# A vision tower on one core: value weights turned a unit sooner, a gate behind the last image's rows, the last tile's output on two queues

## The chip, the cores and the metric

The kernel runs on one core of a Trainium2 chip. The metric is the device time of one execution in microseconds (us). The kernel before was timed in 14 runs: median 732.39 us, from 729.04 to 736.07 us.

The core has five engines with their own instruction streams, each of which is executed strictly in its written order: TensorE (PE in the profile: matrix products and transposes), VectorE (DVE), ScalarE (ACT: activations and copies), GpSimd (POOL: here mostly transfers with row indices) and SyncE (SP: issues transfers). They wait for each other through semaphores. An engine whose next instruction waits holds up everything behind it, though that may be ready.

## The reference

Everything is float32. Four images of 224 x 224 become 784 patches each; the tokenizer gives tokens of 256 numbers, and since query, key and token are the same tokens joined, every row occurs three times (the kernel computes it once). Two layers follow.

```python
h = tokenizer(x)                                    # (4, 3*784, 256)
h = h + L0_attn(layernorm(h))
h = h + L0_ffn(layernorm(h))
h = h + L1_attn(layernorm(h))
h = h + L1_ffn(layernorm(h))

def L0_attn(m):                # attends over the 4 images, for each position and head
    mn = layernorm(m); q, k, v = mn @ Wq, mn @ Wk, mn @ Wv
    g = sigmoid(mn @ Wg + bg)
    att = softmax(einsum('slhc,tlhc->sth', q, k) * scale, axis=1)
    o = einsum('sth,tlhc->slhc', att, v) * g
    return o @ Wo + bo

def L0_ffn(f):                 # 6 experts of three layers, the best 2 of each row
    logits = softmax(relu(f @ router_w1 + router_b1) @ router_w2 + router_b2)
    top_w, top_i = top_k(logits, 2)
    return sum over the two of softmax(top_w) * expert[top_i](f)

def L1_attn(x):                # linear attention: no product of rows with rows
    q, k, v = split(x @ W_qkv + b_qkv)
    q, k = q - mean(q), k - mean(k)
    k2 = l2_normalize(k*k / (sum(k*k) + eps), axis=rows)
    q2 = l2_normalize(q*q / (sum(q*q) + eps), axis=columns)
    return (v + q2 @ (k2.T @ v) / sqrt(N)) @ W_out + b_out

def L1_ffn(x):                 # a shared MLP and the best 2 of 4 small experts
    return shared(x) + sum over the two of weight * expert(x)
```

## The kernel before, in words

**Tiles.** The 784 rows of an image are six tiles of 128 rows and 16 rows left over. The leftovers of all four images share one more tile, number 24 (`LT`), in four bands of 32 partitions. So there are 25 tiles, and `h` (all rows, 256 numbers each) stays on the chip from the tokenizer to the output.

**Order.** Large stretches stand under `tc.manual_schedule`, in which the named engines execute their instructions in the order in which the program writes them. Elsewhere, and for an engine that a stretch doesn't name, a scheduler chooses the order, and it may put such instructions between those of a stretch ordered by hand.

**Layer 0 attention, last image (lines 1575 to 1681).** `s` is image 3, the last; `u` is the unit of six tiles of image 2, whose rows are normalised (`rows_of_part`, line 1025, on ACT), transposed (`turn_part`, lines 311 and 1039) and given to the router while image 3 attends. For image 3, `gate_mm(s, o)` has computed two halves of the gate on PE, `gate_act(s, o)` (line 896) takes their tanh on ACT. The weights of the four images come from `shares_before` and `shares_after` (lines 928 to 937; an exponential on ACT, the rest on DVE). `first_value` (lines 953 and 955) writes the first of four weighted value terms, on the engine that it is given, and `values` (lines 960 and 965) adds the other three and multiplies by the gate, on DVE. The columns are taken in two pieces, the first 512 (`GN`) and the remaining 272 (`rest`). Then `attended` (line 989) multiplies by `Wo` on PE, adds to `h` on DVE and squares on ACT (line 995); `scales_of` takes the roots (line 1004), `shifts_of` the factors on DVE (line 1009).

**Layer 0 experts.** Rows are sent to a table in memory, sorted by expert, by POOL (`send`, line 1154, two transfers a tile), and fetched in blocks of 256 rows (`load`, line 1498). The weights of a block's expert are copied to a buffer (`own_weights`, line 1519, DVE), the block is transposed (line 1528), taken through two layers (`hidden`, line 1543 on PE, line 1549 on ACT) and a third (`rows_back`, line 1561), and stored. Blocks 0 to 6 start while images 2 and 3 are still being routed. `mix1` to `mix3` (lines 1284 to 1295) compute the mixing weights; they are written later, in a stretch that orders DVE, SP and POOL by hand but not ACT.

**Layer 1 attention, start (from line 2207).** Units are three tiles, `LU` is the unit of tile 24 alone. For each unit PE computes q and k (`qk_mm`, line 2001), DVE adds the bias (`qk_add`, line 2007), ACT squares (`qk_squares`, lines 2015 and 2016) and takes roots (`root`, line 2033), DVE makes factors (lines 2039 to 2043) and scales q (`q_rows`, line 2055), ACT scales k (`k_rows`, line 2048). Meanwhile `stats_one` (lines 1767 to 1785) adds the experts' rows to the next unit on DVE, `norm_root` (line 1797) takes its root on ACT, and `norm_rows` (lines 1806 and 1809) normalises on DVE. The value weights never meet the rows directly: `layer1_weights` folds them with `W_out`. It is a generator, run one step at a time with `next(steps)`:

```python
    step 1:  PE transposes Wv (line 812); ACT copies two biases (818) and the result, WvT (819)
    step 2:  PE multiplies WvT by Wout into pwvo (825); ACT copies the two halves to Wvo (829)
    step 3:  PE multiplies the bias (834); ACT copies it (835); DVE adds it to bout (837)
```

Before the change, steps 1 and 2 stand around unit `LU`'s transposes, after all squares of units 0 and 1. `Wvo` is first read by `rows_out` (line 2180).

**Layer 1 experts and output (lines 2326 to 2425).** Seven parts: four of four tiles, then three of three (16 to 18, 19 to 21, 22 to 24). After each part DVE adds the result to `h` (line 2415), and each tile is written to the output three times over (line 2423): 384 KB by SP, or, for the odd tile of the last part, by ACT. Tile 24 goes out as four pieces of 16 rows, one an image.

Of the kernel before, what the change touches and what calls it, by code (L numbers as in the profile page):

```python
# [28 lines left out]
TT = 128  # L29
# [43 lines left out]
def tile_vit_tower(ctx: ExitStack, tc: tile.TileContext, a: dict, out: bass.AP):  # L73
# [819 lines left out]
    def gate_act(s, o):  # L893
        gate = gates[s, o] = attr.tile([P, SEQ], F32, tag="gate", name="gate")
        for i, pg in enumerate(pgs.pop((s, o))):
            nc.scalar.activation(
                gate[:, i * HALF : (i + 1) * HALF], pg, AF.Tanh, bias=bgh[:, o : o + 1], scale=0.5
            )
# [22 lines left out]
    def shares_before(s):  # L921
        if s not in pls:
            shares_mm(s)
        pl = pls.pop(s)
        plv = pl[:, : 2 * NI].rearrange("p (o t) -> p o t", t=NI)
        w = atts[s] = small.tile([P, 2, NI], F32, tag="att", name="att")
        mx = small.tile([P, 2], F32, tag="mx0", name="mx0")
        nc.vector.tensor_reduce(mx, plv, AX.X, ALU.max)
        nc.vector.tensor_tensor(w, plv, mx.unsqueeze(2).to_broadcast([P, 2, NI]), ALU.subtract)
        nc.scalar.activation(w, w, AF.Exp, scale=scale)  # L930
        return mx
# [649 lines left out]
    with tc.manual_schedule(engines=by_hand | {ENG.SP}):  # L1581
        gate_mm(s, 0)
        gate_mm(s, 1)
        products(s, 1, [1])
        expert_weights([2])
        scales_of(u)
        steps = early_blocks()
        next(steps)
        products(s, 1, [2])
        shifts_of(u)  # L1590
        next(steps)
        gate_act(s, 0)
        products(s, 1, [3])
        expert_weights(range(3, E0))
        next(steps)
        mx = shares_before(s)
        next(steps)
        gate_act(s, 1)
        shares_after(s, mx)
    att.close()  # L1600
    work[0] = layer0.enter_context(tc.tile_pool(name="blocks", bufs=2, reuse_waits="tile"))
# [4 lines left out]
    )  # L1606
    with tc.manual_schedule(engines=by_hand | {ENG.SP}):
        first_value(s, 0, 0, GN, nc.vector)
        first_value(s, 1, 0, GN, nc.scalar)
        rows_of_part(u)  # L1610
        values(s, 0, 0, GN)
        for _ in steps:
            pass
        for i in range(4):
            load(i)
        values(s, 1, 0, GN)
        turn_part(u)
        for o in range(2):
            first_value(s, o, *rest, nc.scalar)
        router(u)  # L1620
        values(s, 0, *rest)
        values(s, 1, *rest)
        attended(s, [0, 1])
        keep_left(s)
        attended(s, [2, 3])
        scales_of(ua)
        router_logits(u)
        shifts_of(ua)
        for i in (0, 1):
            b = cols[:, rows[f"eb{i + 1}_0"] :][:, : 2 * E0].rearrange("p (e r) -> p e r", r=2)  # L1630
            nc.vector.tensor_copy(ew[:, :, 6 * D + 2 * i : 6 * D + 2 * i + 2], b)
        attended(s, [4, 5], 0)
        own_weights(0)
        rows_of_part(ua)
        attended(s, [6])
        hidden(0, 0)
        turn_part(ua)
        own_weights(1)
        scales_of(ub)
        choose(u)  # L1640
        turned(1)
        shifts_of(ub)
        rows_of_part(ub, both=True)
        router(ua)
        count(u)
        send(u)
        hidden(0, 1)
        turn_part(ub, both=True)
        router_logits(ua)
        own_weights(2)  # L1650
        hidden(1, 0)
        rows_back(0)
        load(4)
        choose(ua)
        router(ub)
        turned(2)
        hidden(1, 1)
        count(ua)
        hidden(2, 0)
        send(ua)  # L1660
        rows_back(1)
        load(5)
        router_logits(ub)
        own_weights(3)
        turned(3)
        hidden(2, 1)
        choose(ub)
        hidden(3, 0)
        rows_back(2)
        load(6)  # L1670
        own_weights(4)
        count(ub)
        turned(4)
        hidden(3, 1)
        send(ub)
        hidden(4, 0)
        rows_back(3)
        own_weights(5)
        turned(5)
        steps = later_blocks()  # L1680
        hidden(4, 1)
        next(steps)
        hidden(5, 0)
        next(steps)
        rows_back(4)
        next(steps)
        load(7)
        load(8)
        own_weights(6)
        turned(6)  # L1690
        hidden(5, 1)
        next(steps)
        hidden(6, 0)
        next(steps)
        rows_back(5)
        load(9)
        hidden(6, 1)
# [332 lines left out]
    def root(u):  # L2030
        n = units[u][2]
        s4 = sumsof[u][1]
        nc.scalar.activation(s4[:, :n], s4[:, :n], AF.Sqrt, bias=zero[:TT])
# [177 lines left out]
    with tc.manual_schedule(engines=by_hand | {ENG.Pool}):  # L2211
        x_t(1)
        for j in range(UT):
            qk_mm(0, j)
            qk_add(0, j)
            qk_squares(0, j)
        root(0)
        for j in range(UT):
            qk_mm(1, j)
        qk_add(1, 0)  # L2220
        qk_squares(1, 0)
        stats_one(LU, 0)
        norm_root(LU)
        factors(0)
        qk_add(1, 1)
        qk_squares(1, 1)
        norm_rows(LU)
        for b in range(NI):
            nc.gpsimd.tensor_scalar(
                xaM[:, b, :], xaL[:, 0, : D + 2], ofimage[:, b : b + 1], None, ALU.mult  # L2230
            )
        fetch(3)
        qk_add(1, 2)
        qk_squares(1, 2)
        root(1)
        q_rows(0)
        stats_one(2, 0)
        next(steps)
        x_t(LU)
        q_t(0)  # L2240
        k_rows(0)
        next(steps)
        stats_one(2, 1)
        factors(1)
        q_rows(1)
        k_rows(1)
        qk_mm(LU, 0)
        stats_one(2, 2)
        norm_root(2)
        next(steps)  # L2250
        Wvo, bvo = lw[:2]
        q_t(1)
        qk_add(LU, 0)
        qk_squares(LU, 0)
        root(LU)
        norm_rows(2)
        squares[0] = k_squares(0)
        factors(LU)
        fold(0, squares.pop(0))
        k_rows(LU)  # L2260
        squares[LU] = k_squares(LU)
        q_rows(LU)
        squares[1] = k_squares(1)
        fold(1, squares.pop(1))
        k_x_tiles(0)
        x_t(2)
        k_x_left(0)
        kn = k_norm(0)
        fetch(4, kn[:1, :1])
        k_x_out(0, kn)  # L2270
        qk_mm(2, 0)
        qk_add(2, 0)
        qk_squares(2, 0)
        stats_one(3, 0)
        qk_mm(2, 1)
        qk_add(2, 1)
        qk_squares(2, 1)
        q_t(LU)
        gT = g_t(0)
        stats_one(3, 1)  # L2280
        qk_mm(2, 2)
        qk_add(2, 2)
        kv_out(0, gT)
        qk_squares(2, 2)
        stats_one(3, 2)
        normalise(3)
        fetch(5, xa_of(3)[:1, 0, :1])
        rows_out(0)
        x_t(3)
        root(2)  # L2290
        factors(2)
        k_rows(2)
        q_rows(2)
        for j in range(2):
            qk_mm(3, j)
            qk_add(3, j)
            qk_squares(3, j)
            stats_one(4, j)
        squares[2] = k_squares(2)
        qk_mm(3, 2)  # L2300
        qk_add(3, 2)
        qk_squares(3, 2)
        stats_one(4, 2)
        root(3)
        norm_root(4)
        norm_rows(4)
        fetch(6, xa_of(4)[:1, 0, :1])
        parts_ = rows_out_parts(1)
        next(parts_)
        fold(2, squares.pop(2))  # L2310
        factors(3)
        k_rows(3)
        q_t(2)
        x_t(4)
        for done in parts_:
            pass
        q_rows(3)
        squares[3] = k_squares(3)
        fold(3, squares.pop(3))
        behind.append(done.ins.name)  # L2320
# [38 lines left out]
    with tc.tile_pool(name="ffn1", bufs=2) as work:  # L2359
# [3 lines left out]
        for g, tiles in enumerate(parts):  # L2363
# [50 lines left out]
            for j, t in enumerate(tiles):  # L2414
                nc.vector.tensor_tensor(h[:, t, :], pms[j], h[:, t, :], ALU.add)
                b, i = divmod(t, TPI)

                eng = nc.scalar if g == len(parts) - 1 and j % 2 else nc.sync
                cuts = [(b, i * TT, 0, TT)]
                if t == LT:  # L2420
                    cuts = [(k, TPI * TT, k * SEG, LEFT) for k in range(NI)]
                for k, s0, p0, rows_ in cuts:
                    eng.dma_start(
                        out=out[k].rearrange("(k s) d -> s k d", k=REP)[s0 : s0 + rows_],
                        in_=h[p0 : p0 + rows_, t, :].unsqueeze(1).to_broadcast([rows_, REP, D]),
                    )
# [33 lines left out]
```

## Time and profile before

| | us |
|---|---|
| median of 14 runs | 732.39 |
| the profiled execution | 733.89 |
| its span, first to last instruction | 732.2 |
| PE busy in the span | 689.6 |
| DVE busy | 459.5 |
| ACT busy | 332.1 |
| POOL busy | 128.8 |
| mean granted clock of PE | 0.987 |

The profile is of one execution. A timeline line gives the start of an instruction or of several alike (us from the start of the span), how long they took together, the engine, the line of the code, the operation, what it writes and reads, and how many there are; a bracket at its end gives the idle time of the engine just before and what ended it, as far as semaphores show. "issue" stands for a wait for which the profile shows no cause. A matrix product in float32 is recorded as two passes, so eight records are four products. In the table of stretches, a line gives the stretch, its length, the busy time of PE, its weight loads, DVE, ACT and POOL (with the number of instructions begun there), the granted clock of PE, the busy share of the 16 DMA engines and GB/s. The chain of waits goes back from the last instruction, at each step to what released it.

### The profile page before, as it was taken

How to read it: one execution, taken by the hardware profiler on the slowest of the kernel's cores; microseconds unless marked ns; L12 is line 12 of the kernel's file. 1: busy time of each engine (PE TensorE's matmuls, PEld its weight loads, DVE VectorE, ACT ScalarE, POOL GpSimd, SP SyncE). 2: the span in 40 equal slices, each digit the busy share in tenths (PEclk: the TensorE clock that was granted, in tenths of full speed). 3: DMA queues.
4: the chain of work that ended last, by engine and by line, in shares of the span. 5: the costliest groups of instructions: out<-in, count | busy, mean ns of one | idle time of the engine just before them, and what ended most of it. 6: DMA issues, size and time to landing. Idle time of an engine off the chain costs nothing.

```text
span 732.2 us, 9849 instructions
## 1 busy us (share of the span) xinstructions
PE 689.6 (94%) x3043; PEld 477.0 (65%) x3043; DVE 459.5 (63%) x1385; ACT 332.1 (45%) x816; POOL 128.8 (18%) x242
## 2 busy tenths in 40 slices
PE   6899999999997897999999999997999999999996
PEld 4655656566655686788888866664776855555553
DVE  6576775869988733357556668685968654354441
ACT  1665665566797652323332338463545232222231
POOL 6400000000075256200003318453000000000000
PEclk9999999999999899999999999999999999999999
DMA  5999998000037724223234432121000013322333
GB/s 181 313 426 425 425 425 363 0 1 0 1 122 218 278 94 143 96 87 94 94 111 135 120 117 79 55 73 56 1 1 1 4 30 120 118 92 54 115 105 96
DMA packets 56476, 96.49 MB, mean 132 GB/s; under 512 B 6696, under 2 KB 46350, under 8 KB 56424
## 3 DMA queue, kind: packets, MB, share of 16 engines
q1 hardware_dynamic: 49924, 79.69, 30.4%
q0 software_dynamic: 5600, 14.32, 6.5%
q10 hardware_dynamic: 900, 1.86, 0.8%
q8 instruction: 24, 0.39, 0.2%
q14 instruction: 28, 0.23, 0.1%
HBM read 30.75 MB, written 65.09 MB: 131 GB/s over the span
## 4 chain that ended last, share of the span: by engine, by line
PE 58%; DVE 4%; ACT 2%; issue 1%; DVEq 0%; ACTq 0%
PE pb L1543 13%; PE pe L320 6%; PE pyb L1561 6%; PE ps L320 5%; PE pqk L2001 4%; PE ps L2410 3%; PE pukx L2100 3%; PE pout L2180 3%; PE pout L2185 3%; PE pt L311 2%; PE pe L2380 2%; PE ps L2404 2%; PE ptb L1528 1%; PE pkvo L2160 1%; ACT qk L2015 1%
## 5 line engine op out<-in xcount | busy, mean ns | idle before, releaser
L1154 POOL DMA_INDIRECT xrows<-xn,pos x50 | 54.8, 1097 | 212.7 <-DVE nm L1010 172.7
L1753 POOL DMA_INDIRECT ys<-yrows,pos x50 | 49.4, 988 | 134.4 <-DMA yrows<-yb 120.0
L1549 ACT ACTIVATE hb<-pb,own 128x256 f32<-128x256 f32 (+1 forms) x74 | 33.5, 457 | 58.0 <-PE pb L1543 36.8
L1543 PE MATMUL pb<-xTb,own 128*128 128x256 f32 (+1 forms) x240 | 54.5, 371 | 4.9 <-DVE own L1519 2.3
L1543 PE MATMUL pb<-hb,own 128*128 128x256 f32 (+1 forms) x240 | 54.5, 368 | 0.3 <-DVE hb L1551 0.2
L1561 PE MATMUL pyb<-own,hb 128*128 128x256 f32 x216 | 52.3, 381 | 0.3 <-ACT hb L1549 0.2
L1543 PEld LDWEIGHTS pb<-xTb,own 128*128 128x128 f32 x240 | 43.0, 195 | 11.2 <-ACT xn L1025 2.6
L320 PE MATMUL pe<-xT,eW 128*128 128x512 f32 (+1 forms) x112 | 46.0, 553 | 0.0
L2001 PE MATMUL pqk<-Wqkv,lxT 128*128 128x512 f32 x100 | 45.0, 595 | 0.2 <-ACT lxT L94 0.2
L1543 PEld LDWEIGHTS pb<-hb,own 128*128 128x128 f32 x240 | 41.5, 194 | 5.1 <-DVE hb L1551 0.9
L1561 PEld LDWEIGHTS pyb<-own,hb 128*128 128x128 f32 x216 | 40.1, 190 | 6.3 <-ACT hb L1549 1.1
L1567 DVE TENSOR_TENSOR yb<-pyb,eb 128x512 f32<-128x512 f32 (+1 forms) x30 | 19.1, 638 | 37.2 <-PE pyb L1561 31.8
L637 PE MATMUL pw<-Wall,pT 128*128 128x512 f32 (+1 forms) x96 | 42.4, 592 | 0.0
L1532 ACT COPY xTb<-ptb 128x512 f32<-128x512 f32 (+1 forms) x30 | 16.3, 542 | 54.1 <-PE ptb L1528 46.0
L907 DVE SCALAR_TENSOR_TENSOR prod<-kq 128x784 f32<-128x784 f32 x32 | 30.6, 969 | 7.3 <-ACT kq L882 3.9
L320 PEld LDWEIGHTS pe<-xT,eW 128*128 128x128 f32 x112 | 20.2, 190 | 21.6 <-issue 16.5
L1519 DVE COPY own<-kq 128x1540 f32 x30 | 29.2, 976 | 6.6 <-ACT xTb L1532 3.1
L311 PEld LDWEIGHTS pt<-ident,xn 128*128 128x128 f32 x200 | 24.6, 146 | 12.9 <-issue 9.7
L637 PEld LDWEIGHTS pw<-Wall,pT 128*128 128x128 f32 (+1 forms) x96 | 17.9, 189 | 20.5 <-issue 18.5
L2001 PEld LDWEIGHTS pqk<-Wqkv,lxT 128*128 128x128 f32 x100 | 18.6, 192 | 19.4 <-issue 17.5
L1551 DVE TENSOR_SCALAR hb<-pb,own 128x256 f32<-128x256 f32 (+1 forms) x46 | 20.3, 445 | 17.4 <-PE pb L1543 16.5
L311 PE MATMUL pt<-ident,xn 128*128 128x128 f32 x200 | 28.9, 284 | 2.1 <-issue 1.8
(420 smaller groups left out, 1441.1 us busy)
## 6 DMA issues: line engine op xcount, KB each, us to landing
xrows<-nothing SPq DMA_DIRECT2D x22, 896.0 KB
yrows<-nothing SPq DMA_DIRECT2D x22, 896.0 KB
out_dram<-h SPq DMA_DIRECT2D x23, 384.0 KB
xb<-xrows SPq DMA_DIRECT2D x24, 256.0 KB
yrows<-yb SPq DMA_DIRECT2D x24, 256.0 KB
kq<-in_L_ffn_expert_w_dram SPq DMA_DIRECT2D x18, 256.0 KB
wb<-wd SPq DMA_DIRECT2D x16, 128.0 KB
img<-in_x_dram SPq DMA_DIRECT2D x5, 294.0 KB
```

The source lines that it names most:

```text
L311: nc.tensor.transpose(pt[:, j * TT : (j + 1) * TT], xn[:, j, c * P : (c + 1) * P], ident[:TT, :TT])
L320: nc.tensor.matmul(pm[: wcols.stop - wcols.start, :n], w[:, c, wcols], xT(c), start=(c == 0), stop=(c == chunks - 1),)
L637: nc.tensor.matmul(pm, pixels(c, tiles[j]), Wall[: K1[c], c, :], start=(c == 0), stop=(c == 1))
L907: nc.vector.scalar_tensor_tensor(prod, qTs[s][:, o, :], 1.0, kT[:, o, t * SEQ : (t + 1) * SEQ], ALU.mult, ALU.mult, accum_out=atts[s][:, o ...
L1154: put = nc.gpsimd.indirect_dma_start(out=xrows[:, :], out_offset=bass.IndirectOffsetOnAxis(ap=pos[:, k, t0 + j : t0 + j + 1], axis=0), in_ ...
L1519: nc.vector.tensor_copy(w, ewf[0][:, bass.ds(off, EW)])
L1543: nc.tensor.matmul(pm, wm[:, c, o * P : (o + 1) * P], src[:, c, :], start=(c == 0), stop=(c == 1),)
L1549: nc.scalar.activation(dst[:, o, :], pm, AF.Relu, bias=b)
L1561: nc.tensor.matmul(pm[:, t, :], src[:, c, t * P : (t + 1) * P], wm[:, c, :], start=(c == 0), stop=(c == 1),)
L1753: got = nc.gpsimd.indirect_dma_start(out=y[:, j, k, :], out_offset=None, in_=yrows[:, :], in_offset=bass.IndirectOffsetOnAxis(ap=pos[:, k, ...
L2001: nc.tensor.matmul(pqk, xTs[u][:, c, cut(j, 1)], Wqkv[:, c, : 2 * D], start=(c == 0), stop=(c == 1),)
L2100: nc.tensor.matmul(pg, uks[u][:, k, c * P : (c + 1) * P], xas[u % 4][:, k, : D + 2], start=(j == 0), stop=False,)
```

## The change

Three edits. The first moves the second gate of the last image behind the rows of `u` and their transposes, and spreads these rows differently. The second runs steps 1 and 2 of `layer1_weights` earlier: step 1 after unit 0's squares, step 2 after unit 1's products. The third adds a case that cuts the last tile of the last part in two halves, and a line that gives every piece of that tile but the first to ACT. The last tile of the last part is tile 24, `LT`.

```diff
@@ -1593,9 +1593,9 @@
         products(s, 1, [3])
         expert_weights(range(3, E0))
         next(steps)
+        rows_of_part(u, part=(0, 1))
         mx = shares_before(s)
         next(steps)
-        gate_act(s, 1)
         shares_after(s, mx)
...
         first_value(s, 0, 0, GN, nc.vector)
+        rows_of_part(u, part=(1, 4))
         first_value(s, 1, 0, GN, nc.scalar)
-        rows_of_part(u)
+        rows_of_part(u, part=(4, TPI))
         values(s, 0, 0, GN)
         for _ in steps:
             pass
         for i in range(4):
             load(i)
+        turn_part(u)
+        gate_act(s, 1)
         values(s, 1, 0, GN)
-        turn_part(u)
         for o in range(2):
             first_value(s, o, *rest, nc.scalar)
...
             qk_squares(0, j)
+        next(steps)
         root(0)
         for j in range(UT):
             qk_mm(1, j)
+        next(steps)
         qk_add(1, 0)
         qk_squares(1, 0)
...
         stats_one(2, 0)
-        next(steps)
         x_t(LU)
         q_t(0)
         k_rows(0)
-        next(steps)
         stats_one(2, 1)
...
                 if t == LT:
                     cuts = [(k, TPI * TT, k * SEG, LEFT) for k in range(NI)]
+                elif t == parts[-1][-1]:
+                    cuts = [(b, i * TT + p, p, TT // 2) for p in (0, TT // 2)]
                 for k, s0, p0, rows_ in cuts:
+                    if t == parts[-1][-1] and p0:
+                        eng = nc.scalar
                     eng.dma_start(
```

## The prediction

> **What bounds the kernel now.** I read the page first: TensorE (PE) is busy 94% of the span and the chain that ended last lies on it for 58%, so an edit counts only where PE waits for it, or where it moves what PE waits for.
>
> ```profile
> span 732.2 us, 9849 instructions
> PE 689.6 (94%) x3043; PEld 477.0 (65%) x3043; DVE 459.5 (63%) x1385; ACT 332.1 (45%) x816; POOL 128.8 (18%) x242
> PE 58%; DVE 4%; ACT 2%; issue 1%; DVEq 0%; ACTq 0%
> ```
>
> Then the timelines of the three places that the diff touches. Place 1, last image of the attention: ScalarE (ACT) with its second gate ahead of the six rows, then VectorE (DVE), then PE.
>
> ```profile
> 232.53 1.05 ACT L896 ACTIVATE gate<-pg,bgh 128x392 f32<-128x392 f32 x2
> 233.47 0.72 ACT L953 ACTIVATE oT<-vT,att 128x512 f32<-128x512 f32 x1
> 234.08 3.05 ACT L1025 ACTIVATE xn<-h,nm,r 128x256 f32<-128x256 f32 x6
> 240.56 0.94 ACT L953 ACTIVATE oT<-vT,att 128x272 f32<-128x272 f32 x2
> ```
> ```profile
> 239.25 0.69 DVE L965 SCALAR_TENSOR_TENSOR oT<-gate,oT 128x512 f32<-128x512 f32 x1
> 241.13 1.58 DVE L960 SCALAR_TENSOR_TENSOR oT<-vT,att,oT 128x272 f32<-128x272 f32 x3 [1.18 <-issue]
> ```
> ```profile
> 252.44 3.44 PE L1543 MATMUL pb<-xTb,own 128*128 128x256 f32 x8 [2.25 <-DVE own L1519]
> ```
>
> DVE stands 1.18 us before its last value products, until ACT has written their first terms (240.56). From there one string runs: h additions 245.06, ACT squares 245.52, root 249.33, expert weights 251.33, and PE's first expert block at 252.44 after 2.25 us of nothing.
>
> Place 2, start of layer 1: ACT squares two units of rows without a pause, and only then copies the turned value weights, for which PE waits at 447.19.
>
> ```profile
> 440.27 0.30 ACT L2033 ACTIVATE s<-s,zero 128x3 f32<-128x3 f32 x1
> 440.65 0.42 ACT L2015 ACTIVATE qk<-qk 128x256 f32<-128x256 f32 x1
> 442.24 0.30 ACT L1797 ACTIVATE rstd<-mv,eps 128x1 f32<-128x1 f32 x1 [0.29 <-DVE mv L1785]
> 446.57 0.58 ACT L819 COPY WvT<-pwv 128x512 f32<-128x512 f32 x1
> ```
> ```profile
> 443.15 0.60 PE L812 MATMUL pwv<-ident,Wqkv 128*128 128x128 f32 x4
> 447.19 3.68 PE L825 MATMUL pwvo<-Wout,WvT 128*128 128x256 f32 x8 [0.98 <-ACT s L2033]
> 461.50 3.68 PE L2001 MATMUL pqk<-Wqkv,lxT 128*128 128x512 f32 x8
> ```
>
> Place 3, the end: SyncE issues five output DMAs from 726.19 on, and the DMA engines are full until 730.
>
> ```profile
> 726.19 3.58 SPq L2423 DMA_DIRECT2D out_dram<-h  x5
> ```
> ```profile
> 728.00:729.00 1.00, 0.00 (x0) 0.00 (x0) 0.00 (x0) 0.00 (x0) 0.00 (x0) 1.00 0.99 314
> 729.00:730.00 1.00, 0.00 (x0) 0.00 (x0) 0.00 (x0) 0.00 (x0) 0.00 (x0) 1.00 0.99 220
> 730.00:731.00 1.00, 0.00 (x0) 0.00 (x0) 0.00 (x0) 0.00 (x0) 0.00 (x0) 0.82 0.58 152
> ```
>
> **Place 1, step by step.** In the built streams only ACT changes here; DVE, PE, POOL and SP keep their order. ACT is free at 231.66 and waited 0.76 us for the shares' exponential at 232.41; row 0 (0.51 us) fits into that. Rows 1 to 3 then end at 234.06, the first term at 234.7, rows 4 and 5 at 235.7 (24 rows in 12.7 us). PE turns rows as they come, so the four copies (2 x 0.55, 0.65 together) run 235.6 to 237.1. The gate, now behind them, runs to 238.1; its reader on DVE is at 239.25, a margin of 1.1 us. The first terms follow until 239.0, before DVE wants them at 239.9. So the 1.18 us go, and nothing else is late (none of the moved steps issues a DMA): PE's router products start 2 us sooner, half of them at the low clock, and PE's next rows are ready at 243.7 where DVE now comes at 243.9. The string up to PE's block moves by **-1.18**: 251.26.
>
> The streams show one more thing that the diff does not: ACT's later work that no hand orders (exponentials of the mixing weights, L1284, L1285) is scheduled differently. The first now stands between the two halves of the first block's relu, ahead of the root (L1004). That makes two more table loads, 1.28 us each (the load at 258.32 moves up; one is added before the root, one before L1285). ACT has idle time for them: 1.23 us before the second half, 1.98 us before the next block's relu at 265.02. Counting from PE's block, the second half goes from +3.47 to +3.7, the root from +5.1 to +6.6, so DVE's last row ends at +7.85 where the scatter's places were computed at +7.72: +0.16. Rows, router and second layer stay at +7.3, +8.3, +8.9. Bounds: 0 (all in idle time) to 2.57 (both in the open); I take **+0.16**, since the idle rows are longer than the loads.
>
> [...]
>
> After that comes a standstill: DVE waits 7.04 us ("remote") to 278.08, ACT 5.27 us to 278.83, while POOL scatters until 277.0 and PE has nothing. Its end coincides with the end of the scatters, which start from DVE's places at 260.7, so I let the gain through: 0 to -1.02, taken **-1.0**. If the first block also escaped the low clock (clock 0.50 at 253 to 256, 3.44 us for what takes 1.73 elsewhere) it would be -2.7.
>
> **Place 2.** PE transposes the value weights after unit 0's six products instead of after unit 1's, and multiplies them (pwvo) right after unit 1's. That removes the 0.98 us wait and, with PE dense, the low clock (3.68 us against 1.73 for eight such passes): 2.7 us to gain on PE. But ACT must copy them in its own order. Its stream is now: squares of unit 0 (end 440.23), two bias copies, WvT copy (end 441.2), root (441.5), **both Wvo copies (L829), then the squares of unit 1**. The copies wait for pwvo, and pwvo for unit 1's products: 432.85 + 12 x 0.858 + 0.43 for the transposes = 443.58, first half done at 444.45. So ACT stands about 3.0 us, copies at 444.5 and 445.4 (0.37 each), and squares unit 1 from 445.65 instead of 440.65. Queued behind: the root of the left unit (L1797), 442.24 to 446.9. For it DVE waits in norm_rows: its reciprocal goes from 443.32 to 447.2, **+3.88**. Behind that on DVE are the last addition of unit 1, the q rows, three tiles' statistics, factors and q rows of unit 1; DVE was busy 11.76 of 13 us there, so it can't catch up. What it regains is its 1.36 us wait for the bias copy L835 at 453.90, of which 0.66 go (ACT needs root and copy after 456.4: 457.1 against 453.9): +3.22 at the next unit's rows and at the folded sums, which end 463.4 instead of 460.2. PE needed them at 460.69, a slack of 0.5. Its products of unit 2 start at 464.3 instead of 461.50: **+2.8**. On POOL the left unit's masks (L2229) start at 447.85 instead of 446.18, and the three tiles' fetches behind them end at 458.6, early enough for DVE at 467. PE's own way there is shorter (pukx from 455.3 behind q rows, 453.94 before), with 1.3 us to spare for a low clock. Bounds: -2.7 (the stall is hidden, PE keeps its gain) to +3.9 (DVE's whole shift).
>
> **Place 3.** The last tile is the one with the four images' left rows, so the test t == LT comes first and the halves of 64 rows are never cut. What the diff does is send images 1 to 3 (48 KB each) from ACT, behind its 384 KB; nothing else is queued there. SP's issues were at 727.06, 727.46, 727.93 and 729.29, the third taking 1.36; now all are out by about 728.4. But the DMA engines were full to 730 and 0.58 busy after; packing the rest tightly gives 0.2. Bounds: +0.3 (three issues of 0.4 behind ACT's own, last at 728.3, with a 1.36 in it) to -0.9 (the last issue's 1.36 less 0.48). Taken: **-0.2**.
> [...]
>
> **Sum.** -1.0 + 2.8 - 0.2 = +1.6. The profiled execution took 733.89 (span 732.2 and 1.69 around it), 1.50 above the median of the 14 runs. +1.6 makes it 735.5, and the median 732.39 becomes **734.0**.
>
> **Rivals.**
> 1. *The standstill eats place 1* (slower). At 271 to 278 ACT and DVE wait for something that the trace does not name. If its end isn't tied to the scatters, an earlier start buys nothing: 0 + 2.8 - 0.2 = +2.6, 735.0, slower by 0.36%. It decides from the point where DVE's wait grows by as much as its arrival is sooner. For it: no semaphore from POOL stands there. Against: the scatters end 1.1 us before. ACT's longer stream could also lengthen its wait.
> 2. *The stall of place 2 is half hidden.* If the work behind PE at 461 can absorb it, place 2 is 0: -1.2, 731.2. For it: PE reads pwvo's result only at 470. Against: DVE is 90% busy.
> 3. *Place 2 gains as it was drawn*: -1.0 - 2.7 - 0.2 = -3.9, 728.5. It needs ACT to hold unit 1's squares ahead of the copies; the built stream has them behind.
>
> **Chances.** A measurement of this kernel can tell about 0.3% (2.2 us) from no change, and +1.6 lies inside. Forecast 0.56 (its own range 732.6 to 735.6; 0.16 of it above +2.2), rival 1 and what is worse than it 0.24, rival 2 0.10, rival 3 0.10. Faster 0.10, within 0.50, slower 0.40. The range leaves out rival 3 and the worst of the first (both places at their upper ends, +6): 730.6 to 736.8.
>
> **What would show it.** Place 1: the gate behind the xT copies, no wait before L960 on 272 columns, the first pb 1.2 us sooner, loads before L1004 and L1285. Place 2: ACT idle about 3 us before L829, DVE's reciprocal of the left unit waiting 3 to 4 us for ACT, pwvo in 1.7 us, the unit-2 products 2 to 3 us later relative to the first pqk. Place 3: three issues on ACT after 727.03, data ending within 0.3 us of where it did. I am wrong if DVE does not wait there, or if the distance from the first pb to the first pqk changes by over 1 us.

## The result and the profile after

The changed kernel took **744.50 us** (median of 13 runs, 739.69 to 747.43) beside 733.03 us for the kernel before (62 runs): a ratio of 1.0150, 95% interval 1.0134 to 1.0166, some 11 us slower. The forecast was 734.0, its range ended at 736.8, and its sign was right with a chance of 0.40 only.

The page after, the same three lines as before:

```profile
span 739.0 us, 9857 instructions
PE 696.1 (94%) x3043; PEld 479.4 (65%) x3043; DVE 459.4 (62%) x1385; ACT 334.4 (45%) x818; POOL 128.9 (17%) x242
PE 55%; DVE 4%; ACT 3%; another core or an unknown queue 2%; issue 1%; DMA 1%; DVEq 0%; ACTq 0%; SPq 0%
```

PE has the same 3043 records and needs 6.5 us more for them (689.6 before): more of them ran at half clock (between 200 and 520 us a granted clock of 0.50 for 27.3 us, 17.1 before; mean clock 0.980, 0.987 before). ACT has two more instructions, the two table loads, and 2.3 us more of work. The chain now holds waits on DMA and on something unnamed.

To see where the time came from I set every PE instruction's start beside its start before. The difference is 2.3 us ahead of the first changed instruction (1.0 us by 19 us, where the eight products `pwarm` (L532) took 1.92 us, 1.10 before; the rest in a stretch at a granted clock of 0.50, 214.9 to 218.3 us, that the first profile lacks), so the pair can't be read to better than that. From there it goes 2.3, 1.1 (first expert block), 3.4 (end of the router's products), 4.4 (292 us), 6.5 (300), 6.4 (432), 9.0 (461), 6.8 (511), 6.65 (end). The distance from the first expert block to the first products of layer 1, which was to change by less than 1 us, grew by 5.3 us (1.1 to 6.4). The 2.2 us given back at the end of linear attention belong to a standstill of before's profile there (PE waits 1.77 us ahead of 502.57 and 3.47 ahead of 508.31; in after's profile 0 and 3.25; last section). On a quick chip nothing is given back: `after_again` is 3.2 us behind `out_only` at unit 1's first products (431.7 and 428.5 us) and 5.2 at the end of the span (720.5 and 715.3).

**Place 1**, ACT, PE and DVE, and below them the router's products before. In a timeline the bracket is the idle time just before.

```profile
239.41 1.07 ACT L896 ACTIVATE gate<-pg,bgh 128x392 f32<-128x392 f32 x2
240.36 0.94 ACT L953 ACTIVATE oT<-vT,att 128x272 f32<-128x272 f32 x2
...
256.53 1.28 ACT L1284 ACT_TABLE_LOAD   x1
257.82 0.23 ACT L1284 ACTIVATE lg<-lg 128x36 f32<-128x36 f32 x1
...
259.40 1.28 ACT L1004 ACT_TABLE_LOAD   x1
260.69 0.30 ACT L1004 ACTIVATE r<-ss,eps 128x3 f32<-128x3 f32 x1
```
```profile
251.27 0.66 PE L1528 MATMUL ptb<-ident,xb 128*128 128x128 f32 x4 [0.98 <-DMA xb<-xrows]
253.58 1.96 PE L1543 MATMUL pb<-xTb,own 128*128 128x256 f32 x8 [0.78 <-DVE own L1519]
258.94 3.48 PE L320 MATMUL pr<-xT,rw 128*128 128x512 f32 x4 [2.03 <-ACT xT L1039]
```
```profile
242.27 1.57 DVE L960 SCALAR_TENSOR_TENSOR oT<-vT,att,oT 128x272 f32<-128x272 f32 x3
263.60 0.23 DVE L1144 TENSOR_TENSOR sel<-sel,pcount 128x72 f32<-128x72 f32 x1 [1.55 <-PE pcount L1137]
```

Before:

```profile
257.23 1.95 PE L320 MATMUL pr<-xT,rw 128*128 128x512 f32 x4
```

The gate does what was worked out: the first expert block comes 1.19 us sooner against the rest. Then PE waits 2.03 us for the transposed rows, which ACT copies behind the new load, and the router's products run at half clock (3.48 us, the granted clock 0.50 from 259.3 to 262.7; 1.95 us before). PE comes out of them 2.3 us later against the first block: the gain is gone, and as much again. Behind them stand PE's counting products, for which DVE waits with the places of the scatter (L1144): 10.0 us after the first block, 7.7 before.

**Place 2** is as forecast: the wait of ACT for pwvo (3.36 us), of DVE for the left unit's root (3.54), and of PE for its rows (2.50). What stands behind a waiting instruction of ACT waits with it: DVE's first sums of unit 1 are done at 447.5 us (446.79 and 0.69), and ACT squares them at 452.21, behind both copies.

```profile
451.08 0.37 ACT L829 COPY Wvo<-pwvo 128x256 f32<-128x256 f32 x1 [3.36 <-PE pqk L2003]
453.42 0.28 ACT L1799 ACTIVATE rstd<-mv,eps 128x1 f32<-128x1 f32 x1
453.73 0.16 DVE L1808 RECIPROCAL rstd<-rstd 128x1 f32<-128x1 f32 x1 [3.54 <-ACT rstd L1799]
454.40 0.44 PE L311 MATMUL pt<-ident,xaL 128*128 128x128 f32 x2 [2.50 <-DVE xaL L1811]
```

### The profile page after: what moved, and what is told of

Read it like the earlier page. It is cut to its first block, busy times and chain, and to the rows that moved or that the text cites. A ratio compares the mean times of both kernels' runs of the same rounds, so it can differ in the third digit from the quotient of the medians.

```text
span 739.0 us, 9857 instructions
## 1 busy us (share of the span) xinstructions
PE 696.1 (94%) x3043; PEld 479.4 (65%) x3043; DVE 459.4 (62%) x1385; ACT 334.4 (45%) x818; POOL 128.9 (17%) x242
## 4 chain that ended last, share of the span: by engine, by line
PE 55%; DVE 4%; ACT 3%; another core or an unknown queue 2%; issue 1%; DMA 1%; DVEq 0%; ACTq 0%; SPq 0%
PE pb L1543 12%; PE pe L320 6%; PE pyb L1561 5%; PE pqk L2003 5%; PE ps L320 5%; PE ps L2412 3%; PE pout L2182 3%; PE pout L2187 3%; PE pukx L2102 2%; PE pt L311 2%; PE pe L2382 2%; PE ps L2406 2%; PE ptb L1528 1%; PE pkvo L2162 1%
## 5 line engine op out<-in xcount | busy, mean ns | idle before, releaser
L2003 PE MATMUL pqk<-Wqkv,lxT 128*128 128x512 f32 x100 | 46.6, 610 | 0.2 <-ACT lxT L94 0.2
L2017 ACT ACTIVATE qk<-qk 128x256 f32<-128x256 f32 x50 | 20.4, 408 | 22.6 <-DVE qk L2009 20.1
```

The source lines that it names most:

```text
L2003: nc.tensor.matmul(pqk, xTs[u][:, c, cut(j, 1)], Wqkv[:, c, : 2 * D], start=(c == 0), stop=(c == 1),)
```

## The experiments

They ran on five chips (whether the first is among them isn't recorded), and the kernel before is not equally quick on them: 716.3 to 717.2 us on three (called quick here), 733.8 and 737.3 us on two; in the first measurement it took 733.0. Each kernel is compared with the kernel before on its own chip.

| chip, before | kernel | median | ratio, 95% interval |
|---|---|---|---|
| 716.85 | gate_only | 719.23 | 1.0030, 1.0013 to 1.0048 |
| | value_only | 719.88 | 1.0044, 1.0031 to 1.0057 |
| | out_only | 717.02 | 0.9999, 0.9986 to 1.0011 |
| | gate_pinned | 716.28 | 0.9991, 0.9978 to 1.0004 |
| 717.23 | after_again | 723.06 | 1.0087, 1.0072 to 1.0101 |
| | loads_only | 719.42 | 1.0030, 1.0017 to 1.0043 |
| | value_half | 718.15 | 1.0007, 0.9995 to 1.0019 |
| | pinned_half | 718.27 | 1.0016, 1.0003 to 1.0029 |
| 716.27 | loads_only2 | 718.47 | 1.0028, 1.0016 to 1.0039 |
| | gate_only3, after3 (one run each) | 721.13, 725.08 | |
| 733.77 | gate_only2 | 740.19 | 1.0072, 1.0045 to 1.0098 |
| | value_only2 | 735.52 | 1.0019, 0.9995 to 1.0044 |
| | gate_pinned2 | 733.85 | 1.0005, 0.9983 to 1.0027 |
| | after_pinned | 736.85 | 1.0045, 1.0020 to 1.0070 |
| 737.30 | gate_only4 | 737.85 | 0.9992, 0.9977 to 1.0007 |
| | loads_only3 | 735.99 | 0.9985, 0.9971 to 1.0000 |
| | value_late_copies | 738.85 | 1.0017, 1.0000 to 1.0034 |

### Which edit it is

`gate_only`, `value_only` and `out_only` are the diff's three parts, each alone on the kernel before. In `out_only` no tile is cut in halves, though its expectation speaks of them: the test for tile 24 comes first, and only three of that tile's pieces go to ACT.

> Only the first of the three edits: the last image's second gate follows its transposed rows. Theory A (table loads and the clock): the moved gate saves its 1.2 us on VectorE, but ScalarE gets two more table loads of 1.28 us, since the first exponential of the choice now stands between two square roots; the two copies of the transposed rows come 1.7 us later and TensorE spends more 3.4 us stretches at half clock. Most of the change's 11.5 us is here: 6 to 9 us slower than before, about 740 us, and a mean clock of 0.975 to 0.98. Theory B (the terms of the prediction): 1.0 us faster, 732 us. Theory C (value weights cost more than the profiled run shows): within 2 us of before, and the other two edits hold the rest.

> Only the second edit: the value weights of linear attention are turned one unit sooner. The profile of the changed kernel shows the offset grow by 2.5 us between 432 and 465 us, and fall by 2.2 us again by 511 us. Theory A: 0 to 3 us slower. Theory B (the prediction's term): 2.8 us slower, 735.8 us. Theory C: 6 us or more slower, and the profiled run of the changed kernel was a lucky one.

> Only the third edit: the last full tile's output rows leave in two halves by two queues, and the three 16-row pieces with them by ScalarE's queue. All theories: within 0.5 us of before, 733 us; the tail of the changed kernel's profile is 0.15 us longer than that of before. If it is 2 us or more slower, the queue change costs in most executions what the profiled one did not show.

The third edit is worth nothing. The second costs 0.44%, 3.2 us (2.2 to 4.1). The first costs 0.30%, 2.2 us (0.9 to 3.4), where theory B wanted 1 us gained and theory A 6 to 9 lost: A has the sign, not the size. The second is nearest to theory B's 2.8. The changed kernel on a second quick chip:

> The changed kernel itself, once more. Taken alone on a chip where the kernel before takes 716.9 us, the three edits measured +2.4, +3.0 and +0.2 us. If they only add, and the chip decides the rest (theory A2): +5 to +6 us, a ratio of 1.007 to 1.009, where the kernel before takes about 717 us, and +10 to +13 us, a ratio of 1.015, where it takes about 733 us. If the edits are dear together (theory D: the later one meets what the earlier one shifted): +10 us or more on either kind of chip.

1.0087 beside a product of the three ratios of 1.0073: the edits add, and theory D (dear together) falls on the quick chips.

### The table loads

`gate_pinned` is the first edit with the two exponentials put back behind the image's last root:

```diff
         choose(u)
         turned(1)
+        mix1(u)
         shifts_of(ub)
```

(and left out for this unit where they were written). `loads_only` is the opposite, the kernel before with them where the change's build put them (PE and DVE keep before's order of work in it):

```diff
         hidden(0, 0)
-        turn_part(ua)
         own_weights(1)
-        scales_of(ub)
         choose(u)
+        nc.scalar.activation(mixed[u][0], mixed[u][0], AF.Exp)
+        turn_part(ua)
+        scales_of(ub)
         turned(1)
...
         turn_part(ub, both=True)
+        nc.scalar.activation(mixed[u][1], mixed[u][1], AF.Exp)
         router_logits(ua)
```

> The first edit alone, with the two exponentials of the unit's choice written out by hand where they stood in the kernel before (after the last square root of that image), so that ScalarE has as many table loads as before. Theory A: the 1.2 us of the moved gate are kept and the loss is gone: 0.5 to 2 us faster than before, 731 to 732.5 us, at a mean clock of 0.985 or more. Theory B: as the first edit alone, 732 us. A rival (the loss is in the moved rows and gate, or in ScalarE's longer instruction stream, and not in the loads): as slow as the first edit alone, about 740 us.

> The kernel before with one thing changed: the two exponentials of the second to last image's choice are written out by hand at the places where the first edit's build put them, the first ahead of that image's last square root. The gate and the rows stay where they were; two more table loads. Theory A (the loads are the whole price of the first edit, which gains 1.2 us beside): the two loads cost what separates the first edit from its pinned form and more by nothing else, 2 to 4 us slower than before where it takes about 717 us, and 3 to 8 us where it takes about 733 us. The rival (ScalarE's new order around the gate is the price): within 1 us of before.

The loads alone, with the gate untouched, cost 2.2 us (1.0030), as much as the whole first edit; pinned, the first edit costs nothing. So on the quick chips the two loads are its price. Profiles of that place, PE's router products and ACT's copies ahead of them; first the edit alone:

```profile
253.45 1.28 ACT L1284 ACT_TABLE_LOAD   x1
255.24 1.06 ACT L1039 COPY xT<-pt 128x512 f32<-128x512 f32 x2
256.32 1.28 ACT L1004 ACT_TABLE_LOAD   x1
```
```profile
248.20 0.66 PE L1528 MATMUL ptb<-ident,xb 128*128 128x128 f32 x4 [1.09 <-DMA xb<-xrows]
255.87 3.61 PE L320 MATMUL pr<-xT,rw 128*128 128x512 f32 x4 [2.03 <-ACT xT L1039]
```

Then pinned:

```profile
249.16 0.66 PE L1528 MATMUL ptb<-ident,xb 128*128 128x128 f32 x4 [2.10 <-DMA xb<-xrows]
255.27 1.98 PE L320 MATMUL pr<-xT,rw 128*128 128x512 f32 x4 [0.48 <-ACT xT L1039]
```
```profile
254.65 1.05 ACT L1039 COPY xT<-pt 128x512 f32<-128x512 f32 x2
255.59 0.31 ACT L1004 ACTIVATE r<-ss,eps 128x3 f32<-128x3 f32 x1
256.38 1.28 ACT L1284 ACT_TABLE_LOAD   x1
```

The loads alone:

```profile
255.88 1.98 PE L320 MATMUL pr<-xT,rw 128*128 128x512 f32 x4 [1.56 <-ACT xT L1039]
```

And, for neither, `out_only`, which differs from before only at the end:

```profile
255.03 1.98 PE L320 MATMUL pr<-xT,rw 128*128 128x512 f32 x4 [0.28 <-ACT xT L1039]
```

With the load ahead of the copies PE waits 2.03 or 1.56 us (1.80 in `loads_only2`), without it 0.48 or less. With both the moved gate and the load, the products also run at half clock: 3.2 to 3.6 us in all four such profiles from quick chips and in the first one, 1.95 to 1.98 in the four with the gate pinned or the loads alone. On the slower chips `gate_only2` and `gate_only4` have both, and the products take 1.95 and 1.98 us.

The profiles of the loads alone don't show their whole price, for they are of short executions (716.66 and 717.45 us, mean clock 0.995). Beside `out_only`, PE falls 1.1 and 1.6 us behind over place 1. It gets 1.7 us back by 445 us, because `out_only` has a stretch at half clock from 438.2 to 441.6 us (pwvo at 437.68 takes 3.32 us, 1.89 in `value_half`) and they have none there. Of the 24 timed executions of the loads alone on quick chips, the 11 with a mean clock of 0.994 or more took 716.7 to 718.3 us, the 13 with less took 718.7 to 722.6 us. So PE's wait is shown for the loads alone. That the rest of their 2.0 to 2.2 us is stretches at half clock fits these clocks, but no profile shows one.

Also to be seen: the moved gate brings PE earlier to the block's transposes (L1528), and there it waits for the block's transfer, 0.8 to 2.3 us on the quick chips. By PE's starts in `gate_pinned` and `out_only`, 0.5 of the 1.2 us that the gate frees is left at the first block, and 0.1 at the router's products.

### The value weights

`value_half` moves only step 1 (transposes and ACT's three copies) and leaves the products and their two copies where they were:

```diff
             qk_squares(0, j)
+        next(steps)
         root(0)
...
         stats_one(2, 0)
-        next(steps)
         x_t(LU)
```

> Of the second edit only the first half: the transposes of the value weights and ScalarE's three copies of them stand one unit sooner, and the products with the output weights and their two copies stay where they were. Theory V1 (the price is ScalarE's 3.36 us wait for those products, behind unit 1's twelve products on TensorE, with unit 1's squares queued behind it): within 1 us of before. Theory V2 (the price is any copy ahead of unit 0's root): 1.5 to 3 us slower, as the whole second edit.

`value_late_copies` is the second edit with only the two Wvo copies put behind unit 1's root:

```diff
+        yield
+        for c in range(2):
+            nc.scalar.copy(Wvo[:, c, :], pws[c])
         yield
...
         root(1)
+        next(steps)
         q_rows(0)
```

> The second edit alone, with one thing put back: the products of the value weights stay where the edit put them on TensorE, but ScalarE's two copies of their results stand behind unit 1's squares and root. Theory V1 (the second edit's price is unit 1's squares, and the last unit's scale, queued behind ScalarE's 3.36 us wait for those products): the price is gone, within 1 us of before. Rival (the price is the products' place ahead of TensorE's next work): as slow as the second edit alone, +2 to +3 us.

The half costs 0.5 us (0.4 below nothing to 1.4): V1, not V2. In its profile the left unit's root no longer waits for the copies (0.51 us, for DVE), and PE waits 0.91 us for the rows instead of 2.50 (0.23 in `out_only`):

```profile
433.44 0.29 ACT L1797 ACTIVATE rstd<-mv,eps 128x1 f32<-128x1 f32 x1 [0.51 <-DVE mv L1785]
434.44 0.15 DVE L1806 RECIPROCAL rstd<-rstd 128x1 f32<-128x1 f32 x1
435.10 0.44 PE L311 MATMUL pt<-ident,xaL 128*128 128x128 f32 x2 [0.91 <-DVE xaL L1809]
```

With the late copies those waits go altogether, though the products stand early:

```profile
448.34 1.89 PE L827 MATMUL pwvo<-Wout,WvT 128*128 128x256 f32 x8
448.52 0.15 DVE L1810 RECIPROCAL rstd<-rstd 128x1 f32<-128x1 f32 x1
450.07 0.38 PE L311 MATMUL pt<-ident,xaL 128*128 128x128 f32 x2
451.38 0.63 ACT L833 COPY Wvo<-pwvo 128x256 f32<-128x256 f32 x2
452.23 1.98 PE L2005 MATMUL pqk<-Wqkv,lxT 128*128 128x512 f32 x4 [1.01 <-ACT lxT L94]
```

PE now waits 1.01 us for the transposed rows, which ACT copies behind the late copies. The time of this version, 1.3 us above before (0 to 2.5), agrees with V1 within the interval but doesn't exclude its rival, since it ran on another chip than the whole edit. What the trace shows is that the wait belongs to the copies' place on ACT.

### A version that beats both?

> The first edit with its exponentials pinned, and the first half of the second edit; the third left out. Theory A with V1: the moved gate's 1.2 us are kept and nothing is paid: 0.5 to 2 us faster than before. Theory V2: 1 to 2 us slower. Rival (the gate's gain is too small to measure in any form): within 0.5 us.

No. It is 1.1 us slower than before (0.2 to 2.1), and the pinned gate alone is not told from before in two runs (0.9991, 1.0005). Nothing tried is faster beyond the uncertainty; the nearest is `loads_only3`, 0.9985 with an interval up to 1.0000.

### The slower chips

> All three edits, with the two exponentials written out by hand after the image's last square root, so that ScalarE has as many table loads as before. Theory A2 (the edits add): the loads' 2.2 to 3 us go and the value weights' 3 us stay: +2 to +3.5 us where the kernel before takes about 717 us. Where it takes about 733 us, the changed kernel lost 11.5 us; if the loads are most of that too, +3 to +5 us, if not, +8 us or more.

> The first edit alone, again. Where the kernel before takes about 717 us: +2 to +3 us, as measured (ratio 1.003). Where it takes about 733 us: the two profiles from there put the first edit's part of the loss at 4 us (1.2 us gained, 2.3 us at the loads, 1.0 us in a longer standstill of ScalarE, 2.0 us at half clock), so +4 to +8 us; +3 us or less would put the rest of the 11.5 us on the second edit or on the edits together.

> The second edit alone, again. Where the kernel before takes about 717 us: +2.5 to +3.5 us (measured 1.0044). Where it takes about 733 us: +2.5 to +4 us by the two profiles' offset between 432 and 465 us; more than 5 us would put the missing part here.

> The first edit with its exponentials pinned, again: does the moved gate gain anything once the loads are gone? Theory A: 0.5 to 1.2 us faster on either kind of chip (measured 0.9991, not told from 1). Rival: no difference, or slower where the kernel before takes about 733 us, if that chip's standstills take the gain.

Where before takes 733.8 us, the first edit costs 0.72% (5.3 us) and nothing when pinned: again it is what the pinning takes away, at more than twice the price (the loads alone did not run on this chip). The first edit's twelve executions fall into two groups, three at 734 to 735 us and nine at 738 to 742. All three edits with pinned exponentials cost 0.45%, 3.3 us, where the changed kernel had cost 11 us on a chip of the same speed. The second edit alone, expected at 2.5 us or more, costs 1.4 (0.4 below nothing to 3.2). The next kernels were to show the longer executions, and the loads alone, on such a chip:

> The kernel before with the two exponentials ahead of the square root, and so two more table loads, again. Where the kernel before takes about 717 us: +2 to +3 us, as measured. Where it takes about 733 us: theory A, the loads are the price: +5 to +8 us, in two groups of executions as the first edit alone had (734 to 735 us, and 738 to 742 us). Rival (the loads cost their 2 us everywhere, and the rest comes from the moved gate and rows): +1 to +3 us in one group.

> One look at the first edit alone. Where the kernel before takes about 733 us, 9 of 12 executions took 738 to 742 us, and the profiled one was of the faster group. A profile of the slower group should show where its 5 us are. Theory A: between 255 and 300 us, at the two loads and at the standstill of ScalarE that follows (6 us or more ahead of its copy of the turned block, 5.4 us in the faster group), with a stretch at half clock behind it. Rival: in linear attention behind 430 us, where the edit changes nothing.

> One look at the changed kernel. Where the kernel before takes about 733 us, 12 of 15 executions took 744 to 747 us and the profiled one 740.7 us. As for the first edit alone: a profile of the slower group should show 3 to 5 us more than the first profile between 255 and 300 us (theory A), or behind 430 us (rival).

They came to a third quick chip and could not answer that; the loads cost 2.0 us there once more, and the two single executions were 4.9 and 8.8 us above before's median. The two beside each other:

> The kernel before with two more table loads and nothing else. On three runs on faster chips +2.2 us. Where the kernel before takes about 733 us: theory A, +5 to +8 us, as the first edit alone; rival (the rest comes from the moved gate and rows), +1 to +3 us. Where it takes about 717 us: +2.2 us once more.

> The first edit alone, beside the loads alone on the same chip. Theory A: the moved gate gives 0 to 1.2 us back, so it is as slow as the loads alone or up to 1.2 us faster; rival: it is 2 us or more slower than they are.

Here, where before takes 737.3 us, neither costs anything: 0.9985 and 0.9992. **Theory A fails on this chip.** The profile of the first edit alone there is of one of its longest executions (740.9 us). There is no profile of before from this chip. Set beside the first profile of before, its PE is 0.4 us late at 292 us and 7.0 at 300. That is the stretch that theory A named, but not at the loads:

```profile
299.80 0.97 POOL L1154 DMA_INDIRECT xrows<-xn,pos  x1 [0.30 <-issue]
301.86 0.69 DVE L1567 TENSOR_TENSOR yb<-pyb,eb 128x512 f32<-128x512 f32 x1 [9.32 <-PE pb L1543]
302.69 0.58 ACT L1532 COPY xTb<-ptb 128x512 f32<-128x512 f32 x1 [3.94 <-remote]
```

DVE stands 9.32 us and goes on 1.09 us after the last of POOL's scatters (299.80 and 0.97). That is one of the standstills of the last section. The edits move the work that reaches them by 1 to 3 us. Whether that is why the first edit costs 5 us on one such chip and nothing on another isn't shown.

## Why the prediction was wrong

- **Place 1, the gate: right in the trace, small in the time.** No wait before L960, the first block 1.19 us sooner. Alone it is worth 0.6 us (1.6 gained to 0.3 lost) on a quick chip, where PE then waits for the block's transfer; no row of before showed that wait.
- **Place 1, the loads: the step that failed.** "I take +0.16, since the idle rows are longer than the loads", and "Rows, router and second layer stay". ACT's idle time was counted, and DVE's last row followed, but not PE's router products, which wait for the copies behind the first load, nor the counting products and the places behind those. The places were put at +7.9 and the second layer at +8.9 us from the first block; they came at +10.0 and +11.1. (By the prediction's own two figures, +7.85 and +7.72, its term would be +0.13.) Measured: 2.0 and 2.2 us for the loads alone, next to the bound of 2.57. The prediction had noted that the old first block ran at half clock and that escaping it would give time. It did escape (1.96 us, 3.44 before), and the next such stretch fell on the router's products (a granted clock of 0.50 from 252.8 to 256.2 us before, from 259.3 to 262.7 after). Each load takes 1.28 us in these traces and the next instruction follows at once (257.82 behind 256.53, 260.69 behind 259.40).
- **Place 2: right.** +2.8 forecast, 2.5 us between 432 and 461 us in the first pair of profiles; alone, 3.2 us measured on a quick chip (2.2 to 4.1), 1.4 on another (0.4 below nothing to 3.2); waits of 3.36 and 3.54 us where 3.0 and 3.9 were worked out. PE's pwvo ran at the full clock (1.89 us, granted clock 1.00), as drawn, and the stall took more than that. That its new place is why isn't shown: in the old one it took 3.68 us in before, 3.32 in `out_only` and 1.89 in `value_half`. (The gain that it gives as 2.7 us is 2.9 by its rows, 0.98 + 3.68 - 1.73; it was a bound only.)
- **Place 3: right within the uncertainty.** -0.2 forecast, nothing measured, 0.9999.
- **The sum** on a quick chip is 6.2 us (1.0087; 5.2 to 7.2) instead of 1.6. Place 1 is 3.2 of the difference (2.2 lost where 1.0 was to be gained), places 2 and 3 are 0.5; the rest lies within the intervals.
- **The 11 us of the first measurement** hold 5 us more. Of rival 1 the standstill that it named, at 271 to 281, does nothing: it kept its length (7.01 and 5.25 us; 7.04 and 5.27 before). No gain reached it, though. PE came 3.4 us late to it (2.3 of them from ahead of the edits) and left 3.4 us late. But ACT's next standstill grew, 5.76 to 6.76 us, with a block at half clock behind it (3.45 us, the granted clock 0.50 from 296.8 to 300.3):

```profile
281.50 0.21 DVE L1144 TENSOR_TENSOR sel<-sel,pcount 128x48 f32<-128x48 f32 x1 [7.01 <-remote]
282.24 0.84 ACT L1549 ACTIVATE hb<-pb,own 128x256 f32<-128x256 f32 x2 [5.25 <-remote]
295.82 0.59 ACT L1532 COPY xTb<-ptb 128x512 f32<-128x512 f32 x1 [6.76 <-remote]
296.45 3.45 PE L1543 MATMUL pb<-xTb,own 128*128 128x256 f32 x8 [2.97 <-ACT xTb L1532]
```

  That is 3 us of the profiled pair (3.4 to 6.4). Its profiled execution, 740.7 us, is near the lower end of its runs (median 744.5), and there is no profile of a longer one. So another 4 us are not located, and why the first edit costs 0 to 5 us on the slower chips stays open.
- **The range** let the loads reach 2.57 us but took their upper end only together with rare cases, and held nothing for the chip.

## What to carry to other kernels

When an edit changes an order that a scheduler completes, read the whole built stream for instructions that it moved beside those you meant, and pin those that bring table loads with them (here two, 1.28 us each). ACT's idle time did not hide the load that stood ahead of two copies, for which PE then waited 2.03 us: follow each instruction behind a load to its reader, TensorE's first. A copy that waits for a product should not stand ahead of work on its engine that doesn't need it (here 3.36 us, with unit 1's squares behind).

## What the hardware showed

- **Chips of two speeds.** The unchanged kernel takes 716 to 717 us on three chips and 733 to 737 on the others. Each of the five was met once, so that it is the chip and not the hour isn't shown. The profiles show where: set beside a quick chip's, PE in the first profile of before is 1.0 us late at 252 us, 5.0 at 278, 8.8 at 292, 11.6 at 503 and 15.3 at 508. DVE and ACT stand there, and PE behind them. The same instruction, in the kernel before:

```profile
276.03 0.97 POOL L1154 DMA_INDIRECT xrows<-xn,pos  x1 [0.31 <-issue]
278.08 0.20 DVE L1144 TENSOR_TENSOR sel<-sel,pcount 128x48 f32<-128x48 f32 x1 [7.04 <-remote]
```

  and on a quick chip (`out_only`):

```profile
269.80 0.20 DVE L1144 TENSOR_TENSOR sel<-sel,pcount 128x48 f32<-128x48 f32 x1 [0.94 <-PE pcount L1137]
```

  The stands lie in runs of POOL's indirect transfers. Three of them end 1.06 to 1.09 us after the last transfer of a run (278.08, 281.50 and 301.86 against 277.00, 280.44 and 300.77). The quick chips run the same transfers without a stand. In before, no update of PE's semaphore is recorded between 273.06 and 278.06 us, though PE's products run until 275.6; in `out_only` no such gap from 262 to 305 us is longer than 1.9 us. What differs wasn't found, and no run took the transfers away.
- **The clock.** In the profiles of before and after every stretch at a granted clock of 0.50 between 200 and 520 us lasts 3.41 us, one of after's twice that (6.83 us from 235.4). Where they fall differs: before's begin at 235.7, 252.8, 280.1, 447.3 and 508.8 us, after's at 214.9, 235.4, 259.3, 283.2, 296.8, 457.3 and 515.3. The one in place 1 of after follows three waits of PE (0.98, 0.78 and 2.03 us within 9 us). What starts such a stretch isn't shown.
